# Layer 0 of a two-layer kernel: other buffers for the last tile's tokens and for fetched rows, other places for routing, statistics and expert halves

## The chip, the cores and the metric

The kernel runs on one core of one Trainium2 chip. A core has a matrix engine (TensorE, in the profile PE, with its weight loads as PEld), a vector engine (VectorE, DVE), an activation engine (ScalarE, ACT), a general engine (GpSimd, POOL) and a queue engine for transfers (SyncE, SP). Each engine works through its own queue in order. The metric is the device time of one execution in microseconds (us); the profile is of one execution of its own.

## The reference

There are 8 sequences of 512 tokens, 256 wide, all float32, and two layers. Each layer is an attention block and a feed-forward block, both behind a layer norm with a shift and a scale, and both added back through a gate.

```python
# layer 0, attention: a delta rule, one 16x16 state M per sequence and head, token after token
out_t = einsum('bnh,bnhd->bnd', q_t, M)
retrieved = einsum('bnhd,bnd->bnh', M, k_t)
M = M + b_t * einsum('bnh,bnd->bnhd', k_t, v_t - retrieved)
# layer 0, feed-forward: every token goes to the one expert of 8 with the largest logit
top_idx = argmax(x @ gate_w.T + gate_b + expert_bias)
out = w2[top_idx] @ relu(w1[top_idx] @ x + b1[top_idx]) + b2[top_idx]
# layer 1, attention: softmax(q k / 4 + relative bias, causal) v, 16 heads of 16
# layer 1, feed-forward: softmax over 8 experts, those under 0.1 dropped, all experts computed
```

## The kernel before

**Tiles and stages.** The 512 tokens of each sequence are cut into NT = 4 tiles of 128 tokens; a tile i of layer 0 holds 128 tokens of all 8 sequences. For each tile there are four stages.

- `front(i)`: layer norm, projections (L519, L523), silu, `squares` (the sums of squares for the L2 norm, L537 on DVE, waiting for `sq` of ACT, L533), `roots`, `scales` (the multiplications L572 on POOL), and `heads`, which transposes K and V into the order of the scan. Line 572 is in `scales`, lines 580 to 588 in `heads`.
- `scan(i)`: 128 dependent steps on DVE, four instructions each (L625, L629, L635, L640), which update the 128 states of 8 sequences and 16 heads at once. Four scans of this kind follow one another.
- `attend(i)`: what the tile's tokens read from the states: `deltas` (L659, transposes of V after the scan), and for each sequence b `turn`, `scores`, `mask`, `weigh`, `project` (L773, L777), `state`; then for each half h of four sequences `roots` (L804 on DVE, the reciprocal of a root that ACT took at L789), and for each b `rest` (L808, L811, L812, and L813, which stores x1 to memory) and `stats` (L820, L821: the statistics of the second layer norm).
- `route(i)` and `experts(i)`: `route` is a generator in six parts. Its two halves normalise four sequences each (L870, ACT), transpose them (L875), make logits (L893) and the tokens in their own order again (L899, L903). The additions L908, the choice of the expert, the counting matmul L928, the copy L933, the prefix matmuls (L935 to L940) and the comparison L948 follow, up to the slot numbers (L971) and the experts' row numbers `idx` (L980); then eight indirect transfers (L984, POOL) scatter the tokens to `hs`, sorted by expert. `experts` is a generator of 15 slots of 128 tokens in two halves: first half transposes of `hslot` (L1020), the first matmul (L1032) and its activations (L1041); second half the second matmul (L1050), `ysb` (L1055, L1056) and its store to `ys` (L1057). The weights come by indirect transfers on POOL (`fetch`, L1005, 1.05 MB for a first half and 1.18 MB for a second, two buffers for each). After the slots, `gather` (L1065) fetches each token's row back from `ys`; POOL multiplies it with the gate (L1094) and adds it to `x2d` in memory by an accumulating transfer (L1095). These rows lie in `yrow`, two buffers.

**Order.** `run(pieces, steps)` gives the order by hand. Each piece has a number; pieces are emitted in the order of their numbers, pieces with number s after step s of the running scan, and what a piece issues on DVE is put behind that step's L640 (`tc.issue_after`). On the other engines no such edge is set. A planner with costs of its own then fixes each engine's queue: in the trace the reciprocal L804 of the second half, with number 47, ran behind step 49 in scan 3 and step 51 in scan 2, and the zeroing of `v` (L207), emitted after the routing of the last tile, ran between two of its instructions.

While scan i runs, the pieces of `front(i + 1)`, of `attend(i - 1)`, `route(i - 1)` and `experts(i - 1)` run beside it, with those halves of experts that tile i - 2 had left over. `follow(i)` sets these places: the six parts of `route` (38, 47, 56, 61, 63 and 65), and the table `late, pace, starts`: the first `late` slots (10, for tile 2 it is 12) run at 73 + pace * slot in the same scan, a half every pace / 2, the others at `starts` and 3 later in the next. Scan 0 has only `front(1)` and small loads beside it. The last tile (i = 3) has no scan after it: its `attend` and `route` run after scan 3, with the last slots of tile 2 and the gathers of tiles 0 and 1, then its 15 slots with the gathers of tile 2 and with the first pieces of layer 1 (`prologue` of sequence 0: norm L120, transposes L179, values L244, and `both`, L261, the projections of q and k). In that stage the gathers stand at (1, 2.2) and (21, 2.2), which means number 1 and then every 2.2.

**Memory.** Pools take rooms of the on-chip memory one after another. `ap` holds the tiles of the scan and of attention (among them K and V of odd tiles, `terms`, `upd`, `dm`), and is closed in `place1`, where the pool `first1` (`bq`, `v`, `ew`, `qTc`) is opened on the side where other rooms have been given up.

**Layer 1** then goes through the sequences one by one: scores (L1243), bias (L1252), exponential (L1257), transposes (L1269), sums (L1290), with the tail of the sequence before beside it (experts at L1408).

## Time and profile before

| | |
|---|---|
| time, median of 3 runs | 2272.21 us (2269.37 to 2276.05) |
| profiled execution, its own time | 2273.54 us |
| profiled execution, span from the first to the last instruction | 2271.8 us |
| busy in the span | PE 1747.4, PEld 1204.0, DVE 1602.2, ACT 1063.0, POOL 646.9 us |
| mean granted clock of TensorE | 0.874 of full speed |
| first step of scans 0, 1, 2, 3 | at 64.8, 320.8, 588.7 and 869.2 us |
| last instruction of scan 3 on DVE | at 1120.62 us |
| first scores of layer 1 | at 1418.95 us |

The page gives for each engine the busy time, the span in 40 slices of 57 us with the busy share of each slice as a digit, the chain of waits that ended last, and groups of instructions by line. In the timeline a row has start, duration, engine, line, operation, names of what is written and read, the number of merged instructions, and in brackets the engine's idle time before it and what ended it. In the table by stretches, each engine has its busy time and number of instructions. In the list of waits a row has the waiting instruction, what it waited for, the sum, the number of times and the longest.

### The profile page before, as it was taken

Reading aid. Unit: us, or ns where it says so; the run is one execution under the profiler, and the core shown is the slowest. Engines: PE = TensorE matmul, PEld = TensorE weight load, DVE = VectorE, ACT = ScalarE, POOL = GpSimd, SP = SyncE. Lnnn points to the kernel's source line nnn. Section 1 sums busy time; section 2 is a strip of 40 time slices with the busy share of each in tenths; the row PEclk is TensorE's granted clock in tenths of the full one; section 3 lists DMA queues with packets and bytes.
Section 4 is the critical chain, followed back from the end, with each engine's and each line's share of the span. In section 5 each row is a group of like instructions: output and inputs, shape, how many; then the busy total and the mean of one; then the engine's idle time right before and its main releaser. Section 6 shows DMA issues by size and latency. Waiting matters only on the chain. (4 is left out here: it accounts for less than half of the span.)

```text
span 2271.8 us, 32168 instructions
## 1 busy us (share of the span) xinstructions
PE 1747.4 (77%) x10874; PEld 1204.0 (53%) x10874; DVE 1602.2 (71%) x4609; ACT 1063.0 (47%) x2571; POOL 646.9 (28%) x795
## 2 busy tenths in 40 slices
PE   5233026669687896869796787899999999999997
PEld 3212024448566685658775676555555555555553
DVE  3899999889997899999653001676676767666654
ACT  5144024554355543533332233878475666647431
POOL 1102016144472544743326643000102011110111
PEclk9667567689887998979997899899999999999998
DMA  5110000167313583238956884100101010100001
GB/s 160 47 44 9 0 1 10 36 214 278 142 54 98 198 292 121 80 110 317 268 120 162 278 309 141 42 8 15 19 15 24 15 27 12 24 13 13 17 17 17
DMA packets 88628, 214.11 MB, mean 94 GB/s; under 512 B 10872, under 2 KB 64288, under 8 KB 72848
## 3 DMA queue, kind: packets, MB, share of 16 engines
q0 software_dynamic: 33696, 161.98, 22.3%
q1 hardware_dynamic: 54768, 50.09, 7.6%
q8 instruction: 86, 1.41, 0.3%
q14 instruction: 78, 0.64, 0.1%
HBM read 175.10 MB, written 36.93 MB: 93 GB/s over the span
## 5 line engine op out<-in xcount | busy, mean ns | idle before, releaser
L1257 ACT ACTIVATE pr<-sc,low 128x384 f32<-128x384 f32 (+3 forms) x512 | 255.6, 556 | 196.5 <-DVE low L1252 194.2
L1032 PE MATMUL ps<-hTs,w 128*128 128x128 f32 x1920 | 250.7, 293 | 47.6 <-ACT hTs L1024 32.9
L1252 DVE CUSTOM_DVE_ANT_0 sc<-ps,strips 128x384 f32<-128x384 f32 (+3 forms) x512 | 225.4, 485 | 86.7 <-PE ps L1243 55.0
L1032 PEld LDWEIGHTS ps<-hTs,w 128*128 128x128 f32 x1920 | 239.2, 206 | 62.0 <-ACT hTs L1024 48.1
L629 DVE TENSOR_REDUCE state<-terms 128x16 f32<-128x272 f32 x512 | 227.3, 444 | 15.5
L1050 PE MATMUL ps<-w,act 128*128 128x256 f32 x960 | 223.3, 387 | 15.4 <-DMA w<-in_wrows,idx 12.6
L1408 PE MATMUL ps<-ew,hTd 128*128 128x512 f32 x512 | 232.9, 608 | 0.0
L640 DVE TENSOR_TENSOR state<-state,upd 128x256 f32<-128x256 f32 x511 | 220.6, 432 | 17.2
L635 DVE TENSOR_TENSOR upd<-K,state 128x256 f32<-128x256 f32 x511 | 213.9, 419 | 14.9
L1041 ACT ACTIVATE act<-ps,w 128x128 f32<-128x128 f32 x480 | 137.2, 369 | 186.1 <-PE ps L1032 104.7
L625 DVE TENSOR_TENSOR terms<-state,K 128x256 f32<-128x256 f32 x512 | 214.6, 419 | 11.9
L1050 PEld LDWEIGHTS ps<-w,act 128*128 128x128 f32 x960 | 182.1, 194 | 41.1 <-issue 13.9
L1269 PE MATMUL ps<-cst,pr 128*128 128x128 f32 x1280 | 191.5, 295 | 15.2 <-DVE low L1252 12.9
L1413 DVE SCALAR_TENSOR_TENSOR accd<-ps,wtd,accd 128x256 f32<-128x256 f32 x256 | 123.7, 483 | 101.4 <-PE ps L1408 89.5
L1269 PEld LDWEIGHTS ps<-cst,pr 128*128 128x128 f32 x1280 | 149.0, 148 | 83.9 <-DVE low L1252 24.7
L1417 POOL TENSOR_TENSOR accd<-accd,bc_g 128x256 f32<-128x256 f32 x32 | 23.2, 725 | 563.7 <-DVE accd L1413 563.7
L1408 PEld LDWEIGHTS ps<-ew,hTd 128*128 128x128 f32 x512 | 96.4, 193 | 121.2 <-issue 107.6
L1005 POOL DMA_INDIRECT w<-in_wrows,idx x120 | 117.3, 977 | 122.8 <-ACT act L1041 89.7
L1243 PE MATMUL ps<-kT,qTc 32*128 32x384 f32 (+3 forms) x1024 | 131.5, 492 | 6.3 <-DVE low L1252 4.4
L1278 DVE COPY prT<-ps 128x512 f32<-128x512 f32 (+3 forms) x256 | 117.0, 484 | 10.3 <-PE ps L1269 9.9
L725 POOL TENSOR_TENSOR stk<-stk,cst 128x512 f32<-128x512 f32 x96 | 119.3, 1270 | 17.1 <-ACT stk L724 15.1
L1276 ACT COPY prT<-ps 128x512 f32<-128x512 f32 (+3 forms) x256 | 99.0, 414 | 8.6 <-PE ps L1269 8.2
(252 smaller groups left out, 2878.7 us busy)
## 6 DMA issues: line engine op xcount, KB each, us to landing
hs<-zero SPq DMA_DIRECT2D x4, 1920.0 KB
hslot<-hs SPq DMA_DIRECT2D x60, 128.0 KB
ys<-ysb POOLq DMA_DIRECT2D x60, 128.0 KB, 3.1
x<-in_x SPq DMA_DIRECT2D x32, 128.0 KB
strips<-strip_d SPq DMA_DIRECT2D x16, 256.0 KB
out<-accd POOLq DMA_DIRECT2D x32, 128.0 KB, 3.1
wm<-in_wmod SPq DMA_DIRECT2D x4, 768.0 KB
xt<-in_x SPq DMA_DIRECT2D x12, 256.0 KB
```

Of the source, the lines that this page charges most:

```text
L625: nc.vector.tensor_mul(term[:, :, :HD], M, K[:, s, :].unsqueeze(1).to_broadcast([P, HD, HD]))
L629: nc.vector.tensor_reduce(delta, term, AX.X, ALU.add)
L635: nc.vector.tensor_mul(upd, K[:, s, :].unsqueeze(2).to_broadcast([P, HD, HD]), delta.unsqueeze(1).to_broadcast([P, HD, HD]),)
L640: yield nc.vector.tensor_sub(M, M, upd).ins
L1032: nc.tensor.matmul(ph[:, q * P : (q + 1) * P], w[:, k * FF + f * P : k * FF + (f + 1) * P], hT[:, k, :], start=(k == 0), stop=(k == 1),)
L1041: nc.scalar.activation(act[:, f, :], ph[:, q * P : (q + 1) * P], AF.Relu, bias=w[:, 2 * FF + f : 2 * FF + f + 1],)
L1050: nc.tensor.matmul(py[:, :D], act[:, f, :], w[:, f * D : (f + 1) * D], start=(f == 0), stop=(f == NFC - 1),)
L1243: made = nc.tensor.matmul(pscs[r][:, :W], qT[rows, g, o, i * P : (i + 1) * P], kT[rows, g, :W], start=True, stop=True,)
L1252: nc.vector.tensor_tensor_reduce(out=sc[:, :W], in0=pscs[r][:, :W], in1=strips[:, n, S - W :], scale=1.0, scalar=3.0e38, op0=ALU.add, op1= ...
L1257: nc.scalar.activation(pr, sc[:, :W], AF.Exp, bias=low, scale=-1.0)
L1269: nc.tensor.transpose(pt[:, (i - j) * P : (i - j + 1) * P], prs[r, i][:, j * P : (j + 1) * P], ident,)
L1408: nc.tensor.matmul(pe, hT[0][:, k, cols], ew[:, k, e : e + 2, :], start=(k == 0), stop=(k == 1),)
```

## The change

The numbers of pieces move. In `front`, for tiles 1 to 3, `squares` goes from +11 to +14 and `roots` and `scales` from +23 to +27; `heads` goes from 46 and 49 to 49 and 52. In `attend`, for tiles 0 and 1, `rest` and `stats` of the second half come 2 later and its `roots` 4 later. In `follow`, for tiles 0 and 1, the six parts of `route` go from (38, 47, 56, 61, 63, 65) to (38, 49, 59, 65, 69, 72), the first slot from 73 to 77, and the halves of left-over slots get places of their own, for tile 2 as well. The rows that are fetched back for tiles 0 and 1 go to eight parts of one buffer `fetched`, in the room of K, and the multiplication follows three gathers later and not one. For the last tile, the normalised tokens go to two scratch tiles in the rooms of `upd` and `dm`, and the tokens that are scattered to the room of `terms`, where both were written over x1. The two pieces `both` of the first three tiles of layer 1 go from 126 and 130 to 151 and 152.

```diff
@@ -600,13 +600,13 @@
                     late = 4.5 if i == 0 else 0
                     pieces.append((at + 8 * p + 3 * c + 4 + late, lambda b=b: project(b)))
-                    pieces.append((at + 8 * p + 3 * c + 11, lambda b=b: squares(b)))
+                    pieces.append((at + 8 * p + 3 * c + (14 if i else 11), lambda b=b: squares(b)))
             for h in range(B // n):
-                last = at + 16 * h + (23 if i else 39)
+                last = at + 16 * h + (27 if i else 39)
                 pieces.append((last, lambda h=h: roots(h)))
                 pieces.append((last + 2, lambda h=h: scales(h)))
-            pieces.append((at + 46, lambda: heads("K", qk[:, 1])))
-            pieces.append((at + 49, lambda: heads("V", v)))
+            pieces.append((at + 49, lambda: heads("K", qk[:, 1])))
+            pieces.append((at + 52, lambda: heads("V", v)))
             got["qk"] = qk
             return got, pieces
@@ -834,12 +834,15 @@
                     pieces.append((5 * b + 9, lambda b=b: state(b)))
                 pieces.append((5 * b + 8 + later, lambda b=b: project(b)))
             for h in range(2):
-                pieces.append((20 * h + 27, lambda h=h: roots(h)))
+                wait = 2 * h if i < NT - 2 else 0
+                pieces.append((20 * h + 27 + 2 * wait, lambda h=h: roots(h)))
                 for b in range(4 * h, 4 * h + 4):
-                    pieces.append((18 * h + 28 + b, lambda b=b: rest(b)))
-                    pieces.append((16 * h + 32 + b, lambda b=b: stats(b)))
+                    pieces.append((18 * h + 28 + wait + b, lambda b=b: rest(b)))
+                    pieces.append((16 * h + 32 + wait + b, lambda b=b: stats(b)))
             return got, pieces
+        DEPTH = (3, 3, 1, 1)
         issued = {}
@@ -859,6 +862,22 @@
                 return x.unsqueeze(1).to_broadcast([P, n, x.shape[1]])
             lg = grid("lg")
+            xn, made = h, h
+            if i == NT - 1:
+                xn = [
+                    ap.tile([P, HD, HD], F32, tag="upd", name=f"xnf{b}").rearrange(
+                        "p a b -> p (a b)"
+                    )
+                    if b % 2
+                    else ap.tile([P, 2, P], F32, tag="dm", name=f"xnf{b}").rearrange(
+                        "p a b -> p (a b)"
+                    )
+                    for b in range(2)
+                ] * (B // 2)
+                room = ap.tile([P, STEPS, HD, HD + 1], F32, tag="terms", name="h_last")
+                room = room.rearrange("p s a b -> p (s a b)")
+                made = [room[:, b * D : (b + 1) * D] for b in range(B)]
             for half in range(2):
                 rs, off = scale_offset(fp, "f", *norms[half])
                 pl = bank()
@@ -866,9 +885,9 @@
                 for n in range(5):
                     b = 4 * half + n
                     if n < 4:
-                        hb = h[b]
+                        hb = xn[b]
                         nc.scalar.activation(
-                            hb, hb, AF.Identity, bias=off[:, n : n + 1], scale=rs[:, n : n + 1]
+                            hb, h[b], AF.Identity, bias=off[:, n : n + 1], scale=rs[:, n : n + 1]
                         )
                         pt = bank()
                         for c in range(2):
@@ -900,9 +919,9 @@
                                 back[:, c * P : (c + 1) * P], turned[:, c, :], ident
                             )
                         if i == NT - 1:
-                            nc.vector.tensor_copy(h[b - 1], back[:, :D])
+                            nc.vector.tensor_copy(made[b - 1], back[:, :D])
                         else:
-                            nc.scalar.copy(h[b - 1], back[:, :D])
+                            nc.scalar.copy(made[b - 1], back[:, :D])
                     turned = hT
                 yield
                 nc.vector.tensor_add(
@@ -984,7 +1003,7 @@
                 issued["scatter"] = nc.gpsimd.indirect_dma_start(
                     out=hs_views[b],
                     out_offset=bass.IndirectOffsetOnAxis(ap=slot[:, b : b + 1], axis=0),
-                    in_=h[b],
+                    in_=made[b],
                     in_offset=None,
                 ).ins
             yield slot, idx
@@ -1082,17 +1101,24 @@
                         nc.gpsimd.dma_start(x2d[b][i], rows[b], accum_op=ALU.add)
                 yield
                 return
+            if i < NT - 2 and "fetched" not in w1:
+                fetched = ap.tile([P, P, HD], F32, tag="K", name="fetched")
+                w1["fetched"] = fetched.rearrange("p t d -> p (t d)")
             queue = []
-            for b in range(B + 1):
+            for b in range(B + DEPTH[i]):
                 if b < B:
-                    yr = fp.tile([P, D], F32, tag="yrow", name=f"yrow{i}_{b}", bufs=2)
+                    if i < NT - 2:
+                        yr = w1["fetched"][:, b * D : (b + 1) * D]
+                    else:
+                        yr = fp.tile([P, D], F32, tag="yrow", name=f"yrow{i}_{b}", bufs=2)
                     with tc.issue_after(issued["scatter" if i == NT - 2 else "fetch"]):
                         gather(b, yr)
                     queue.append(yr)
-                if b > 0:
-                    yr = queue.pop(0)
-                    nc.gpsimd.tensor_mul(yr, yr, gates[1][:, b - 1, :])
-                    nc.gpsimd.dma_start(x2d[b - 1][i], yr, accum_op=ALU.add)
+                if b >= DEPTH[i]:
+                    yr, k = queue.pop(0), b - DEPTH[i]
+                    nc.gpsimd.tensor_mul(yr, yr, gates[1][:, k, :])
+                    nc.gpsimd.dma_start(x2d[k][i], yr, accum_op=ALU.add)
                 yield
         def follow(i, qk, V):
@@ -1115,24 +1141,28 @@
             def on():
                 next(work["experts"])
-            pieces += [(38, begin), (47, more), (56, more), (61, more), (63, more), (65, settle)]
-
-            late, pace, starts = {
-                NT - 1: (0, 4, [10 * j for j in range(NSLOT)]),
-                NT - 2: (12, 4.3, [58, 68, 71]),
-                NT - 3: (10, 4.6, [10, 26, 44, 50, 66]),
-            }.get(i, (10, 4.6, [10, 26, 42, 58, 70]))
+            places = (38, 49, 59, 65, 69, 72) if i < NT - 2 else (38, 47, 56, 61, 63, 65)
+            pieces += zip(places, (begin, more, more, more, more, settle))
+            first, late, pace, starts = {
+                NT - 1: (0, 0, 4, [(10 * j, 10 * j + 3) for j in range(NSLOT)]),
+                NT - 2: (73, 12, 4.3, [(54, 64), (66, 67), (68, 69)]),
+                NT - 3: (77, 10, 4.6, [(9, 12), (22, 25), (35, 38), (58, 61), (70, 73)]),
+                NT - 4: (77, 10, 4.6, [(8, 11), (20, 23), (32, 35), (60, 63), (67, 70)]),
+            }[i]
             rest = []
             for j in range(NSLOT):
                 for half in range(2):
                     if j < late:
-                        pieces.append((73 + pace * (j + half / 2), on))
+                        pieces.append((first + pace * (j + half / 2), on))
                     else:
-                        rest.append((starts[j - late] + 3 * half, on))
+                        rest.append((starts[j - late][half], on))
             if i == NT - 1:
                 rest += [(200, on), (250, on)]
             at, apart = [(1, 2.2), (21, 2.2), (100, 2), (0, 0)][i]
-            return pieces, rest, [(at + apart * n, on) for n in range(B + 1)]
+            return pieces, rest, [
+                (at + apart * n, on) for n in range(B + DEPTH[i])
+            ]
         def load1():
@@ -1218,7 +1248,8 @@
         begun = list(prologue(0, first, w1["xs"], (tuple(range(NT - 1)), (NT - 1,))))
         for k, piece in enumerate(begun):
-            last.append((102 + 4 * k if k < NT + 4 else 201 + k, piece))
+            place = 102 + 4 * k if k < NT + 2 else 145 + k if k < NT + 4 else 201 + k
+            last.append((place, piece))
         run(last)
     rec.close()
```

## The prediction

> **What bounds the kernel now.** I read the table by stretches first, cut at the starts of scans 1, 2 and 3, at the end of scan 3 and at layer 1's first scores.
>
> ```profile
> core 0: us, PE busy (x) PEld busy (x) DVE busy (x) ACT busy (x) POOL busy (x), PEclk, DMA share, GB/s
> 320.80:588.70 267.90, 188.14 (x1214) 147.47 (x1213) 243.18 (x634) 132.40 (x324) 116.50 (x140) 0.80 0.39 135
> 588.70:869.20 280.50, 226.20 (x1528) 185.40 (x1527) 243.82 (x634) 142.94 (x371) 134.88 (x164) 0.89 0.44 154
> 869.20:1120.90 251.70, 197.04 (x1458) 168.38 (x1457) 232.27 (x592) 99.96 (x295) 121.68 (x141) 0.89 0.51 171
> 1120.90:1418.90 298.00, 232.88 (x1643) 198.80 (x1641) 56.02 (x146) 100.57 (x305) 142.88 (x166) 0.89 0.68 204
> ```
>
> In the scans DVE is the bound: 232 to 244 us busy, and scan 2 takes 12.6 us more than scan 1 for the same 634 instructions. Scan 3 has fewer of them. In the fourth stretch, 298 us, no engine is full, so a chain of waits sets the time. Layer 1 (853 us, PE busy 817) isn't touched; it starts earlier or later.
>
> Second view: the waits of DVE alone between 320 and 1120 us, which is what each scan loses.
>
> ```profile
> DVE ss L537 <- ACT sq L533: 12.0, 2, 6.4
> DVE ms L804 <- ACT ms L789: 11.4, 4, 7.0
> DVE lg L908 <- PE ps L893: 5.4, 2, 3.0
> DVE count L933 <- PE ps L928: 3.3, 2, 2.8
> ```
>
> With L948 (1.0) and L820 (0.5) that is 33.6 us. By scan, from the timeline of DVE: scan 1 L908 2.99, L933 0.53, L537 5.61, so 9.1; scan 2 L804 1.02 and 7.02, L820 0.46, L908 2.41, L933 2.80, L948 0.98, L537 6.42, so 21.1; scan 3 L804 1.20 and 2.16, so 3.4. In all of them DVE is in its queue too early for a result of PE and ACT, and the whole scan stands behind it.
>
> Third view: groups of POOL from 1131 to 1237 us, then three timelines of the same stage, for PE, DVE and POOL.
>
> ```profile
> L1065 POOL DMA_INDIRECT yrow<-ys,slot x16 | 16.9, 1054 | 25.8 <-DMA x<-yrow 25.1 <-issue 0.8
> L1095 POOL DMA_DIRECT2D x<-yrow x16 | 15.1, 966 | 5.4 <-POOL yrow L1094 4.0 <-issue 1.5
> L1094 POOL TENSOR_TENSOR yrow<-yrow,gate 128x256 f32<-128x256 f32 x16 | 13.0, 811 | 23.1 <-DMA yrow<-ys,slot 23.1
> ```
> ```profile
> 1205.50 1.18 PE L875 MATMUL ps<-cst,x 128*128 128x128 f32 x4 [11.59 <-ACT x L870]
> ...
> 1212.88 5.16 PE L1032 MATMUL ps<-hTs,w 128*128 128x128 f32 x32
> 1217.87 3.62 PE L1050 MATMUL ps<-w,act 128*128 128x256 f32 x16
> 1221.42 0.43 PE L928 MATMUL ps<-cst,pick 128*64 128x128 f32 x2
> ```
> ```profile
> 1225.23 0.22 DVE L980 TENSOR_SCALAR idx<-of,cst 128x15 uint32<-128x15 f32 x1
> ```
> ```profile
> 1237.03 1.00 POOL L984 DMA_INDIRECT hs<-x,slot  x1 [0.30 <-issue]
> ```
>
> POOL spends 106 us on 16 gathers, 54.3 us of them idle, nearly all waiting for one of two `yrow` buffers to be read or filled. So the scatter, ready at 1225.45, starts 11.6 us late. Ahead of it PE stood idle for 11.59 us before the second half of the routing and then ran two expert halves (8.6 us) between the logits and the count that the slot numbers need. Last, PE at the end of the stage:
>
> ```profile
> 1380.62 2.74 PE L261 MATMUL ps<-hTc,wqkv 128*128 128x384 f32 x8
> 1387.97 2.75 PE L261 MATMUL ps<-hTc,wqkv 128*128 128x384 f32 x8
> ...
> 1412.39 0.69 PE L179 MATMUL ps<-cst,xnc 128*128 128x128 f32 x2 [10.15 <-ACT xnc L172]
> ```
>
> The slots of the last tile follow one another there on PE without a wait (8.07 us each), and the two projections lie between them, while 10.15 us of idle stand behind the last slot.
>
> **The change, part by part.** The sum is made against the profiled execution's own 2273.54 us (span 2271.8 and 1.7 around it), which is 1.3 over the median.
>
> *A, places in the scans.* All stalls of scan 1 and those of scan 2 but the first L804 lie behind pieces that move: 9.1 + 20.1 = 29.2 us. A step is 1.91 us (290.2 to 305.5 for 8 steps). The second L804 comes 4 steps later, 7.6 against a stall of 7.02: gone. The additions L908 have six steps instead of five after the half that feeds them, 1.9 more against 3.0 and 2.4; I leave 1 us in each scan, +2. The copy L933 has 4 steps instead of 2, L948 3 instead of 2: both gone. `squares` comes 3 steps later, 5.7 against 5.6 and 6.4, and the last projection (number 78) no longer has three expert halves ahead of it but one, since the slots start at 77: gone.
>
> What comes back: in scans 2 and 3 two more expert halves stand before `project` of the fourth sequence (number 25): 8, 11, 20, 23 against 10, 13, and 9, 12, 22, 25 against 10, 13. Two halves are 8.2 us of PE (L1020 0.38, L1032 3.84, L1050 3.62 and gaps), and L804, just behind, has 1.0 and 1.2 us of stall already, with PE idle for about 2.5 us in that place in which part of it fits. The price is between 0 (the planner puts L804 as much later, as it did in scan 2, step 51 for number 47) and 8.2 in each scan; I take 3 and 2, near the rows of the present stall, because DVE has steps to run meanwhile: +5.
>
> The slots start later than at 77: the routing ends 7 steps later, 13.4 us, and the scatter (8 times 1.28) and the fetch stand behind that. In scan 1 the first L1032 goes from 480.4 to 480.4 + 13.4 - 3.5 (earlier stalls) = 490.3; the chain of ten slots lasted 97.6 us to 577.95 with two projections in it (4.5 each with their gaps), which now run before it: 490.3 + 88.6 = 578.9. PE needs V at 587.61 - 9.1 + 1 = 579.5. The 9.66 us that PE idled there are used up: no stall, but no cover; +1. In scan 2 the same sum ends 2 to 3 us ahead. `heads`, 3 steps later, end near step 104 of 128: 24 steps, 46 us of cover; the nearest wait, PE for POOL's `qk`, moves with it. A = -29.2 + 2 + 5 + 1 = -21, between -29 and -6.
>
> *B, routing of the last tile.* The first half of slot 12 (54) now stands before the second half of the routing, in the 11.59 us of idle; the second half (64) behind the prefix matmuls. The count then doesn't wait for 5.16 + 3.62: DVE had its operand at 1215.0, so 1221.42 becomes 1215.1, -6.3. If the tokens of slot 12 come late (they were issued at 1200.1 behind the stores of x1 on SP), L1032 runs in front of the routing instead and up to 5 us of this are lost. With eight places and a distance of three, POOL's own work is 16.9 + 15.1 + 13.0 + 32 issues of 0.3 = 54.6 us: free at 1132.4 + 55 = 1187 without waits, near 1200 if half of the 23.1 us for rows stays. From issue to landing these transfers took 2.7 to 14.6 us, median 4.1; three in flight at 3.4 us of POOL each cover 10. The second tile's gathers wait for the first tile's accumulation out of the same place, eight gathers or 27 us earlier: 0. Behind a gather that waits stand, on POOL, the fetches for slots 13 and 14 and the scatter. The first gather now waits for K's last reader (1119.7; it ran at 1132.43): 0.
>
> Ahead of the scatter stay on POOL the addition, store and fetch of slot 12, which follow L1050 (now 1216.6 to 1220.2): the scatter at 1224 instead of 1237, -13; with the risk of slot 12, -12. Behind it, slots 13 and 14 (PE to about 1237) and the first slot of the last tile (1255.68 - 12) still fit.
>
> [...]
>
> *Scratch and `terms`.* The normalisation needn't wait any more for the store of x1; but that L870 was ended by DVE's offset (1204.70), so 0. The third L870 of a half waits for the first transposes (0.6): +1 at most, in the risk above. `terms` is held until the scatter has read it, and `first1` may lie over it. Then the zeroing of `v` (L207, 1.76 us twice, which stood between the reciprocal and the offset of this routing) comes later, up to -3.5, and the loads of `ew`, 2 MB that ran at 1201 to 1210 at 301 GB/s, fall among the fetches of the last tile, whose first slots already waited 10.2 us for weights: up to +7. I take +3.
>
> *C.* Two `both` leave the row of slots: -2.74 - 2.75, and run in the 10.15 us of idle, beside ACT, which is idle too: -5.5, between -5.5 and -3 if they wait for ACT.
>
> Sum: -21 - 12 + 3 - 5.5 = -35.5; 2273.5 - 35.5 = 2238, at the median 1.3 less: 2236.5 us.
>
> **The rivals.** *The stalls come back at the front (0.14).* L804 of the first half takes the full 8.2 in scans 2 and 3, and L908 keeps its stall: A = -29.2 + 16.4 + 5 + 2 = -6, and the time 2252. For it: the granted clock of 0.8 to 0.89, which stretches PE's work. Against it: the longest such stall behind two halves was 7.0, the one at number 27 1.2.
>
> *The routing gains nothing (0.12).* The gathers go on waiting, or slot 12 is in front: B = 0 and the loads of `ew` +5: 2273.5 - 21 - 5.5 + 5 - 1.3 = 2250.5. This is also the case in which the change doesn't do what it says, one buffer in eight parts being treated as one. Against it: the eight gathers into parts of `rows` were issued 1.25 us apart at 1406.6 to 1415.4.
>
> *Slower (0.10).* The slots of tiles 0 and 1 run past the end of scans 1 and 2, and `deltas`, with all of `attend`, queues behind them. The lateness for each scan is 13.4 + 20 (ten slots at the 2 us of weight wait that the first five of the last tile had) - 9.66 = 24 us, 48 in all: 2284. It decides from 35.5 / 2 = 18 us for each scan. Against it: these slots followed one another at 8.07 us without a wait.
>
> **How the numbers follow.** Forecast 0.62; 0.14, 0.12 and 0.10 for the rivals; 0.02 for anything else. Its own best is A -29, B -16, C -5.5: 2221.5; its worst, with the first two rivals in part, is A -6, B -6, C -3, loads +5: -10, near 2262. The range is 2219 to 2262. A measurement here tells 0.3% (6.8 us) from no change: faster by that (under 2265.4) 0.84, within it 0.06, slower 0.10.
>
> **What would show it.** Right: scan 2 within 3 us of scan 1 with the waits for `sq` gone; the 16 gathers done by 1200 less the scans' gain; the scatter within 4 us of `idx`; L261 of 384 columns in the idle behind the last slot. Wrong: a wait at the first L804 over 5 us in scans 2 or 3; `deltas` behind slots in scan 2 or 3; L1032 of slot 12 directly before L875; waits of PE for weights over 15 us in the last tile's first five slots.

## The result, and the profile after

| | before | after |
|---|---|---|
| time, median of 7 runs each, in turn | 2270.58 us (2266.4 to 2277.12) | 2279.41 us (2276.44 to 2288.84) |
| ratio, with its 95% interval | | 1.0045 (1.0024 to 1.0066): slower |
| profiled execution, span | 2271.8 us | 2278.8 us |
| last step of scan 3 ends | 1120.1 us | 1138.2 us |
| first `deltas` of the last tile to layer 1's first scores | 288.2 us | 280.8 us |
| layer 1, from its first scores to the end | 852.8 us | 847.7 us |

The scans lost 18.1 us, the stage behind them won 7.4. Layer 1's 5.1 us are no part of it: over all profiles shown here it took 839.2 to 856.0 us with the same instructions.

In the kernel after, the lines from `route` on stand lower: L875 is L894, L893 L912, L908 L927, L928 L947, L933 L952, L948 L967, L980 L999, L984 L1003, L1005 L1024, L1020 L1039, L1032 L1051, L1050 L1069, L1056 L1075. The table by stretches of after, cut at its own scan starts (columns as before):

```profile
321.00:586.70 265.70, 185.56 (x1206) 144.92 (x1205) 242.35 (x634) 134.72 (x325) 114.41 (x137) 0.81 0.36 126
586.70:869.90 283.20, 216.79 (x1510) 177.80 (x1509) 242.60 (x633) 143.81 (x368) 134.01 (x163) 0.90 0.43 149
869.90:1138.40 268.50, 201.91 (x1476) 172.80 (x1475) 231.82 (x591) 101.79 (x301) 125.05 (x145) 0.85 0.51 172
1138.40:1431.10 292.70, 232.66 (x1651) 197.40 (x1649) 57.80 (x147) 100.77 (x305) 143.08 (x167) 0.90 0.70 210
```

DVE is as busy as before in each scan (242, 243, 232 us), so what the scans grew by is waiting: scan 3 takes 268.5 us instead of 251.7. The waits of DVE in the scans of after (waited for: sum, times, longest):

```profile
DVE ms L804 <- ACT ms L789: 16.6, 3, 8.0
DVE count L952 <- PE ps L947: 9.6, 2, 5.0
DVE dm L800 <- POOL bdM L801: 5.9, 3, 2.4
DVE ss L537 <- ACT sq L533: 5.1, 1, 5.1
DVE over L967 <- PE ps L959: 4.7, 2, 3.1
DVE ss L554 <- ACT ss L550: 4.6, 2, 3.3
```

Before had 12.0 us at L537, 11.4 at L804, 5.4 at L908 and 3.3 at L933. L537 and the logits shrank (L927, the old L908, has 3.4 us now), L804, the counting copy and the comparison (L967, before 1.0) grew, and two waits are new: L800 for POOL's state addition, and L554 (in `scales`) for the root of ACT.

Behind scan 3, the timelines of PE, DVE and POOL of after:

```profile
1220.04 0.69 PE L1039 MATMUL ps<-cst,hslot 128*128 128x128 f32 x2 [11.32 <-DMA hslot<-hs]
1221.19 6.31 PE L1051 MATMUL ps<-hTs,w 128*128 128x128 f32 x32 [0.46 <-ACT hTs L1043]
1227.34 0.60 PE L894 MATMUL ps<-cst,xnf 128*128 128x128 f32 x4
...
1276.57 0.69 PE L1039 MATMUL ps<-cst,hslot 128*128 128x128 f32 x2 [14.13 <-DMA hslot<-hs]
...
1423.95 0.69 PE L179 MATMUL ps<-cst,xnc 128*128 128x128 f32 x2 [5.00 <-ACT xnc L172]
```
```profile
1240.12 0.23 DVE L999 TENSOR_SCALAR idx<-of,cst 128x15 uint32<-128x15 f32 x1
```
```profile
1240.50 1.04 POOL L1003 DMA_INDIRECT hs<-h_last,slot  x1 [10.47 <-DVE idx L999]
```

POOL now waits for `idx` (10.47 us) and not the other way round: the scatter starts 0.15 us after it, as forecast. Slot 12 stands in front of the routing, with PE waiting 11.32 us for its tokens and computing 6.31. Even so `idx` is ready 90.0 us after the stage's first `deltas`, where it took 94.6 before, and the scatter starts after 90.2 us instead of 106.2. But the last tile's first slot then waits 14.13 us for its own tokens and starts after 126.3 us instead of 123.7.

### The profile page after: what moved, and what is told of

It is laid out like the page before. It is cut to its first block, busy times and chain, and to the rows that moved or that the text cites. A ratio compares the mean times of both kernels' runs of the same rounds, so it can differ in the third digit from the quotient of the medians.

```text
span 2278.8 us, 32182 instructions
## 1 busy us (share of the span) xinstructions
PE 1737.3 (76%) x10874; PEld 1193.4 (52%) x10874; DVE 1601.6 (70%) x4609; ACT 1070.3 (47%) x2576; POOL 647.0 (28%) x795
## 5 line engine op out<-in xcount | busy, mean ns | idle before, releaser
L1051 PE MATMUL ps<-hTs,w 128*128 128x128 f32 x1920 | 245.4, 289 | 46.7 <-ACT hTs L1043 37.2
L1051 PEld LDWEIGHTS ps<-hTs,w 128*128 128x128 f32 x1920 | 233.9, 203 | 62.0 <-ACT hTs L1043 53.7
L1069 PE MATMUL ps<-w,act 128*128 128x256 f32 x960 | 225.4, 389 | 16.7 <-DMA w<-in_wrows,idx 14.1
L640 DVE TENSOR_TENSOR state<-state,upd 128x256 f32<-128x256 f32 x511 | 220.8, 432 | 17.2
L1069 PEld LDWEIGHTS ps<-w,act 128*128 128x128 f32 x960 | 183.1, 196 | 41.8 <-issue 12.3
L1300 PE MATMUL ps<-cst,pr 128*128 128x128 f32 x1280 | 188.1, 291 | 15.5 <-DVE low L1283 12.1
L1300 PEld LDWEIGHTS ps<-cst,pr 128*128 128x128 f32 x1280 | 146.0, 146 | 84.1 <-DVE low L1283 24.6
L1024 POOL DMA_INDIRECT w<-in_wrows,idx x120 | 117.3, 977 | 168.8 <-ACT act L1060 139.4
L1274 PE MATMUL ps<-kT,qTc 32*128 32x128 f32 (+3 forms) x1024 | 131.6, 488 | 4.0 <-DVE low L1283 2.4
```

Source lines behind the costliest of these rows:

```text
L640: yield nc.vector.tensor_sub(M, M, upd).ins
L1051: nc.tensor.matmul(ph[:, q * P : (q + 1) * P], w[:, k * FF + f * P : k * FF + (f + 1) * P], hT[:, k, :], start=(k == 0), stop=(k == 1),)
L1069: nc.tensor.matmul(py[:, :D], act[:, f, :], w[:, f * D : (f + 1) * D], start=(f == 0), stop=(f == NFC - 1),)
L1274: made = nc.tensor.matmul(pscs[r][:, :W], qT[rows, g, o, i * P : (i + 1) * P], kT[rows, g, :W], start=True, stop=True,)
L1300: nc.tensor.transpose(pt[:, (i - j) * P : (i - j + 1) * P], prs[r, i][:, j * P : (j + 1) * P], ident,)
```

## The experiments

All kernels start from the diff's two sides and take some of its edits. The table collects what the traces of the main ones say: stalls are DVE's idle times over 0.3 us within a scan, "stage" is the time from the last tile's first `deltas` to layer 1's first scores. Each ratio is to the kernel before, measured beside it on the same chip.

| kernel | ratio (95%) | stalls in scans 1, 2, 3 | end of scan 3 | stage |
|---|---|---|---|---|
| before | | 9.1, 21.1, 3.4 | 1120.1 | 288.2 |
| after | 1.0045 (1.0024 to 1.0066) | 7.8, 24.6, 20.5 | 1138.2 | 280.8 |
| scans_only | 1.0067 (1.0042 to 1.0093) | 7.4, 24.4, 20.7 | 1136.8 | 289.4 |
| post_only | 0.9955 (0.9931 to 0.9979) | 8.9, 22.2, 5.5 | 1123.2 | 285.0 |
| scans_old_starts | 0.9967 (0.9941 to 0.9993) | 5.1, 12.9, 5.1 | 1110.5 | 289.4 |
| scans_starts_only | 1.0095 (1.0060 to 1.0129) | 7.8, 27.0, 16.2 | 1138.4 | 290.2 |
| change_old_starts | 0.9918 (0.9890 to 0.9946) | 5.3, 12.9, 4.6 | 1111.1 | 290.7 |
| starts_early | 1.0047 (1.0022 to 1.0072) | 7.4, 27.5, 9.2 | 1130.1 | 291.3 |
| starts_second | 1.0055 (1.0034 to 1.0075) | 8.1, 22.3, 12.1 | 1129.9 | 296.0 |
| starts_third | 1.0002 (0.9978 to 1.0027) | 8.1, 20.3, 5.9 | 1122.8 | 295.5 |
| warm_change | 1.0039 (1.0011 to 1.0066) | 5.2, 24.1, 17.2 | 1130.7 | 282.1 |
| rows_only | 0.9941 (0.9919 to 0.9963) | 8.0, 16.2, 4.6 | 1117.1 | 276.7 |
| both_only | 0.9945 (0.9920 to 0.9970) | 8.2, 13.0, 6.0 | 1115.8 | 285.5 |
| rows_both | 0.9917 (0.9888 to 0.9946) | 8.5, 20.3, 5.5 | 1125.0 | 271.2 |
| post_no_made | 0.9935 (0.9911 to 0.9959) | 8.4, 21.0, 5.5 | 1127.8 | 278.8 |

Stalls, end and stage come from one profiled execution of each kernel, and they vary. Seven kernels have all numbers in the scans as before (before, post_only, rows_only, both_only, rows_both, post_no_made and rows_both_64); their stalls are 8.0 to 9.1, 13.0 to 22.2 and 3.4 to 6.1 us. Seven have everything behind scan 3 as before (before, scans_only, scans_old_starts, scans_starts_only and the three starts_ kernels); their stages are 288.2 to 296.0 us. A difference inside such a spread shows nothing by itself.

**The two sides of scan 3.** scans_only has the edits to `front`, `attend` and the scans' part of `follow`; post_only the rest: slot 12's numbers, `fetched` with `DEPTH`, the scratch and `terms`, and `both`.

> The numbers of the scans alone (front, second half of attend, route, slots from 77, left-over slots); behind scan 3 all as before. First theory: the whole loss of scan 3 (17 us more stalls) and the slots that end behind scan 2 come from these numbers, so +16 to +20 us, about 2289, with scan 3 ending near 1139. Rival: the stalls of scan 3 come from what the planner makes of the pieces behind it, then under +8, about 2277.

> The changes behind scan 3 alone (eight places for the fetched rows at a distance of three, scratch and room of terms for the last tile, slot 12 at 54 and 64, both at 151 and 152); all numbers of the scans as before. First theory: the scans lost some 18 us and the last stage won, so here scan 3 ends at 1121 and the time is 7 to 12 us under the kernel before, about 2261. Rival: the last stage won only because the scans came late and the transfers beside it were done by then; then it stays within 3 us of the kernel before, about 2271.

Measured: 1.0067 and 0.9955. The places in the scans cost, the edits behind them gain, and the loss is larger than the gain.

**The numbers of the left-over halves.** Two theories: the new places of the halves that tile i - 2 left over crowd the early part of a scan; or the first ten slots, which start at 77 and later, run into the next scan.

```diff
 # scans_old_starts: scans_only, but (scans_starts_only is before with only the "-" lines' numbers)
-  NT - 3: [(9, 12), (22, 25), (35, 38), (58, 61), (70, 73)],
-  NT - 4: [(8, 11), (20, 23), (32, 35), (60, 63), (67, 70)],
+  NT - 3: [(10, 13), (26, 29), (44, 47), (50, 53), (66, 69)],
+  NT - 4: [(10, 13), (26, 29), (42, 45), (58, 61), (70, 73)],
 # change_old_starts: the whole change with the same two lines put back
```

> As scans_only, but the left-over slots of tiles 0 and 1 keep their numbers of before (10, 13, 26, 29, 42 or 44, ...); front, attend, route and the first slot at 77 moved. Theory late slots: scan 3's stalls come from slots that start at 77 and run past the end of scan 2, so deltas and all of attend start 6 us late; then scan 3 keeps 15 us or more of its 20.7 us of stalls, about +12. Theory left-over slots: they come from four halves before number 25 and six before 45; then scan 3 falls back to 3 to 7 us and the time to within 4 us of the kernel before.

> Only the left-over slots of tiles 0 and 1 at their new numbers, all else as before. Theory late slots: scan 3 stalls 3 to 7 us, time within 4 us of the kernel before. Theory left-over slots: scan 3 stalls 12 to 20 us, about +12, with the waits at L804 of the first half, the logits and the count, and deltas at once after the scans.

> The whole change, with the left-over halves of the first two tiles at their old numbers. If those numbers alone carry the loss, the stalls of scans 1, 2, 3 fall from 7.8 + 24.6 + 20.5 us to about 5 + 13 + 5, scan 3 ends 25 to 28 us earlier than in the kernel after, and the time is 2250 to 2256 us, ratio 0.992: the change turns from slower to faster by one table. If the loss came from the meeting of the scan places with what was added behind them (gathers, scratch, terms), stalls over 15 us stay in scans 2 and 3 and the time is 2268 us or more.

With the old numbers scan 3 falls from 20.7 to 5.1 us of stalls and scan 2 from 24.4 to 12.9; with only the new ones, 16.2 and 27.0 stand there. Scan 3 shows it best: in after its 20.5 us are 3.78 at the first L804, 3.75 at L800, 3.10 at the logits, 4.87 at the second L804 and 5.03 at the count, and in change_old_starts only the second L804 is left, with 4.55. And the whole change with two lines of its table put back is 0.8% faster than before instead of 0.45% slower. Its first ten slots still start at 77: they carry no loss. (Its profiled execution was the slowest of its six, 2270.1 us beside a median of 2256.8, so of that trace I read the scans and not the stage.) scans_starts_only lost 0.95%, some 22 us, more than the 12 expected, and its first L804 in scan 3 waited only 0.96 us. The wait that the late pair (58, 61) makes, in PE and DVE in scan 3 of scans_starts_only:

```profile
1008.16 5.23 PE L1051 MATMUL ps<-hTs,w 128*128 128x128 f32 x32
1013.22 3.62 PE L1069 MATMUL ps<-w,act 128*128 128x256 f32 x16
1016.77 0.43 PE L947 MATMUL ps<-cst,pick 128*64 128x128 f32 x2
```
```profile
1017.24 0.28 DVE L952 COPY count<-ps 64x128 f32<-64x128 f32 x1 [4.61 <-PE ps L947]
```

Both halves, 8.85 us of PE, went between the last logits and the counting matmul, where before PE was idle and the count came at once. It is the same pattern that the prediction had found, and priced at 6.3 us, in the last tile.

**Which half.** Before, with some of the new numbers alone: starts_early the first three pairs of each row, starts_second the second pair, starts_third the third.

```diff
 # starts_second                                          (starts_third)
-  NT - 3: [(10, 13), (26, 29), (44, 47), (50, 53), (66, 69)]
+  NT - 3: [(10, 13), (22, 25), (44, 47), (50, 53), (66, 69)]   # third: (26, 29), (35, 38)
-  NT - 4: [(10, 13), (26, 29), (42, 45), (58, 61), (70, 73)]
+  NT - 4: [(10, 13), (20, 23), (42, 45), (58, 61), (70, 73)]   # third: (26, 29), (32, 35)
```

> Before, with only the first three left-over slots of the first two tiles at the new numbers (8 to 38); the last two at the old ones (50, 53 and 66, 69; 58, 61 and 70, 73). If the loss comes from halves crowded ahead of the first half's projections and roots (numbers 20 to 38), the waits of DVE at the first reciprocal, at delta's multiplication and at the logits stay, some 11 of the 16.2 us of scan 3, only the wait at the slot comparison (4.6) goes, and the time is 2280 or more. If it is the halves at 58 to 63, in front of the counting, scan 3 falls to about 5 us and the time to within 5 of before.

> Before, with only the second left-over slot of tiles 0 and 1 earlier: (20, 23) and (22, 25) for (26, 29). The prediction's +5 came from this crowding (two more halves ahead of number 25). By it the first reciprocal waits longer in scans 2 and 3, 1.0 and 1.2 us become 2 to 5 each, and the time is some 5 us over before. If what is late is POOL (multiplication with the gate, ysb, store and fetch in one queue with the state additions), the wait stands at the statistics and at delta's multiplication of scan 2, steps 32 to 34, some 4 us, and the first reciprocal's goes. If the third slot carries all, the time is that of before.

> Before, with only the third left-over slot of tiles 0 and 1 earlier: (32, 35) for (42, 45) and (35, 38) for (44, 47). If a half in the steps 35 to 45 pushes the routing's matmuls and the state additions of POOL behind it, scan 3 gets the waits at delta's multiplication, the logits and the second reciprocal (some 8 to 9 us instead of 3.4), and scan 2, whose second reciprocal waited 7.0 us behind this very slot at its old place, gets no better (20 to 24). Time 5 to 8 us over before. If it is only freed of the slot in front of the roots, scan 2 falls to 14 and the time to 5 us under before.

Moving the second pair alone costs 0.55%, the third nothing that can be told, the three early pairs 0.47%, all five 0.95%. By subtraction about half of the loss is the second pair's and half that of the two last ones; but the intervals are wide, the two last pairs were not run alone, and of their share the traces show the 4.61 us at the count. What the second pair does stands in two views of starts_second, POOL's timeline in scan 2 and one line of DVE's:

```profile
655.10 1.43 POOL L811 TENSOR_TENSOR y<-y,gate 128x256 f32<-128x256 f32 x2
656.47 1.41 POOL L812 TENSOR_TENSOR x<-x,y 128x256 f32<-128x256 f32 x2
657.83 1.11 POOL L813 DMA_DIRECT2D x<-x  x2
658.96 0.73 POOL L801 TENSOR_TENSOR bdM<-bdM,dm 128x256 f32<-128x256 f32 x1
```
```profile
659.73 0.42 DVE L800 TENSOR_TENSOR dm<-ps,cst 128x256 f32<-128x256 f32 x1 [2.19 <-POOL bdM L801]
```

The planner put the reciprocal L804 behind step 31 instead of 27, and there it waits for nothing. But the multiplications, additions and stores that follow it (L811 to L813 for four sequences) came 4 steps later too, in POOL's queue, directly ahead of a state addition L801 (number 29), and the next L800 (number 34) stops the scan for 2.19 us, 2.21 in scan 3. Before, the same L801 stood behind them too, but it ended at 656.06, and L800 ran at 657.62 without a wait. In scan 3 L804 itself, at step 30, waits 2.42 as well, against 1.20 before. These three waits are 6.8 us of the 12 that the pair costs; where the rest is lost this trace doesn't show. I had expected the wait at L804 or at L800; it is at both. The starts_third theory of waits at the logits and at delta's multiplication held in scan 3 only for the logits (1.86 us), and its second reciprocal waited 3.52, which is no more than the 2.16 to 6.06 that it waits in the kernels with the old numbers; neither of the two times expected came.

**Is it the clock?** The same order of instructions need not give the same stalls. Over the first 75 steps of scan 2 the queues of PE, DVE, ACT and POOL have the same order in before, rows_only and both_only. DVE stalled there 14.7, 6.5 and 6.6 us, all of it in steps 24 to 75, and in these steps the granted clock stood at half for 41.0, 22.1 and 22.2 us. The half of a slot that the prediction's 7.0 us wait stood behind, in before and in both_only:

```profile
684.89 6.32 PE L1032 MATMUL ps<-hTs,w 128*128 128x128 f32 x32 [0.46 <-ACT hTs L1024]
```
```profile
679.54 3.84 PE L1051 MATMUL ps<-hTs,w 128*128 128x128 f32 x32 [0.52 <-ACT hTs L1043]
```

The second L804 then waits 7.02 us in before and 0.98 in both_only. All five kernels with the new second pair and no matmuls added have 41.0 us of half clock there, and after has 58.0 in the same steps of scan 3 (before 33.3). That made the clock a theory for the whole loss: halves that run early leave PE idle later, and the routing then runs at half clock. Opposite to it stands the queue: the halves are simply in front. warm_change adds matmuls to the change that nothing reads; warm_best adds them to best_front (below).

```diff
 # in route, each half of tiles 0 to 2: two behind the first transposes of half 0, four ahead of half 1
+  nc.tensor.matmul(pl, ident, cst[:, C_ID : C_ID + 512], start=True, stop=True)
```

> The whole change, with matmuls added that nothing reads (128x512, 1.11 us each at full clock): two behind the first transposes of the routing's first half, four ahead of its second half, for tiles 0 to 2. They lie where TensorE stood idle (3.5 and 6.6 us in scan 2, 13.6 us in scan 3). If the scans' stalls come from a TensorE that runs at half clock after such idle, the time at half clock in steps 24 to 75 falls from 41 us (scan 2) and 58 us (scan 3) to about 25 and 45, the stalls there from 18.2 and 20.5 us to about 8 and 13, and the time is near 2262 although TensorE has more to do. If the stalls come from work queued ahead on TensorE or GpSimd, the stalls stay or grow by the 2.2 us that were added, and the time is 2279 to 2285.

> front's numbers, eight places for rows, both in the idle, slot 12 at (58, 64), no scratch, and the same matmuls that nothing reads. If the clock sets the stalls, scan 2 loses about half of its 13.8 us in steps 24 to 75 and the time is 5 to 8 us under the same kernel without them (2248.8 beside a before of 2277), ratio 0.985 to 0.987. If not, it is the same or 2 to 4 us over it, 0.989 to 0.990.

The 23.9 us from 683.7 on, in which PE's clock was at half in after, in the table by stretches of after and of warm_change:

```profile
683.70:707.60 23.90, 19.81 (x92) 15.14 (x93) 14.81 (x43) 12.15 (x30) 8.95 (x11) 0.50 0.06 17
```
```profile
683.70:707.60 23.90, 19.43 (x106) 12.20 (x107) 19.04 (x58) 12.92 (x34) 10.97 (x15) 0.79 0.11 34
```

The clock did what the theory says: 0.79 instead of 0.50, half clock down from 41.0 to 23.9 us in scan 2 and from 58.0 to 40.5 in scan 3, and the second L804 waits 1.79 and 1.31 us instead of 7.96 and 4.87. The time didn't: 1.0039 against 1.0045, where 2262 us were expected and 2281.6 measured. The waits of DVE in warm_change, its lines from `route` on 10 lower again:

```profile
DVE count L962 <- PE ps L957: 10.0, 2, 5.4
DVE ms L804 <- ACT ms L789: 8.3, 4, 4.1
DVE dm L800 <- POOL bdM L801: 6.1, 3, 2.5
```

Count and L800 wait as long as ever, and the logits wait 2.04 and 2.19 us (0 and 3.10 in after). In steps 24 to 75 the stalls are 17.3 and 17.2 us instead of 18.2 and 20.5, while rows_only and change_old_starts, with about as much half clock (22.1 and 40.2, 19.5 and 36.8 us), have 6.5 and 4.6, and 5.5 and 4.6. So the clock decides how long the second L804 waits, but it isn't the cause of the whole loss; that theory fell. A smaller share isn't excluded: the two intervals leave room for some 9 us, the added matmuls may cost some time of their own, and in this profile scan 3 ends 7.5 us earlier than in after, while layer 1 takes 8.3 more. warm_best, 0.9890 (0.9846 to 0.9934) against 0.9884 for the same kernel without the matmuls, decides nothing: the 0.985 to 0.987 that the clock theory asked for lies inside its interval.

**Behind scan 3.** rows_only has `fetched` and `DEPTH` alone, both_only the new numbers of `both`; rows_both has these two, post_no_made slot 12's numbers as well. rows_both_64 is rows_both with slot 12's second half later.

```diff
-  DEPTH = (1, 1, 1, 1)                 # rows_only, rows_both
+  DEPTH = (3, 3, 1, 1)                 # with the eight places in the room of K
-  102 + 4 * k if k < NT + 4            # both_only, rows_both
+  102 + 4 * k if k < NT + 2 else 145 + k if k < NT + 4
-  NT - 2: [(58, 61), (68, 71), (71, 74)]
+  NT - 2: [(54, 64), (66, 67), (68, 69)]   # post_no_made; rows_both_64: (58, 64)
```

> Before, with only the eight places for fetched rows and the distance of three. POOL is then done with its 16 gathers some 20 us sooner and the scatter starts at idx, 11.6 us earlier against it: the stretch from deltas to layer 1's first scores is 276 to 278 us and the ratio 0.995. If the fetches of the last tile's weights, not the scatter, set the first slot, the stretch shrinks by less than 5.

> Before, with only the two projections of layer 1's second and third tile moved to 151 and 152. The prediction's part C by itself: 5.5 us from the stretch between the deltas of the last tile and layer 1's first scores (288.1 us), so 282 to 283 there and a ratio of 0.9976. If they only change places with other work, 288 and 1.0.

> Of the changes behind scan 3 only the eight places for fetched rows at a distance of three, and both at 151 and 152; no scratch, no room of terms, slot 12 at 58 and 61 as before; the scans as before. First theory: the scatter starts when idx is ready (-11.6 us), the slots of the last tile begin 9 to 12 us earlier, both saves 5: about 2257. Rival: the first slots of the last tile wait for their weights as long as the transfers before them take, and only both is won: about 2266.

> The changes behind scan 3 without the scratch tiles and the room of terms for the last tile's tokens; the scans as before. First theory: the pool of layer 1's first tiles no longer waits for the scatter, the 2 MB of ew load before it and not in front of the last tile's first hslot, so 8 to 12 us under post_only. Rival: the first slot waits for the fetches of weights, not for ew, and the time is that of post_only within 3 us.

> As rows_both, but slot 12 of tile 2 has its first half at 58 as before and its second at 64, behind the prefix matmuls, and slots 13 and 14 follow at 66 to 69. If the second matmul of slot 12 (3.6 us) is what holds the count up, the scatter comes 3 to 4 us earlier against deltas than in rows_both and the time is 3 us less; if the first slot of the last tile waits for its weights and not for the scatter, it is the same within 2 us.

rows_only shortens the stage from 288.2 to 276.7 us, 11.5, with the scatter right behind `idx`, and the time by 0.59%; the stage lies clear of the spread and the ratio's interval clear of 1. both_only's stage is 2.7 us shorter, and from rows_only to rows_both it is 5.5; its time fell by more (0.55%), but its scan 3 ended 4.3 us earlier and its layer 1 took 7.8 less with nothing changed there, so I don't put that down to the edit. With slot 12's new numbers the stage is 7.6 us longer (271.2 to 278.8), though the scatter starts as early (97.6 and 96.9 us after the first `deltas`); with (58, 64) it is 273.6 and the ratio 0.9921 (0.9888 to 0.9953), no better than 0.9917. With the scratch and `terms` it is 6.2 us longer still (278.8 in post_no_made, 285.0 in post_only). None of the steps of 2.7 to 7.6 us is clear of the spread (rows_both_front, with the edits of rows_both behind scan 3, has 276.7), and the times 0.9917, 0.9935 and 0.9955 don't tell these kernels apart.

What does stand out is the stretch from the scatter to the end of the stage's last second matmul. It is 173.2 to 178.6 us in the four kernels with the scratch and `terms` (after, post_only, change_old_starts, warm_change) and 156.9 to 167.9 in the sixteen without; the last tile's first slot waits 12.0 to 14.9 us in the four and at most 6.4 in the others. The two loads of `ew` on SP, in before and then in after, and PE's wait for that slot in before:

```profile
1201.17 1.34 SPq L212 DMA_DIRECT2D ew<-in_expert_w  x2
```
```profile
1253.86 1.01 SPq L212 DMA_DIRECT2D ew<-in_expert_w  x2
```
```profile
1254.53 0.69 PE L1020 MATMUL ps<-cst,hslot 128*128 128x128 f32 x2 [6.41 <-DMA hslot<-hs]
```

In before these loads were issued 36 us ahead of the scatter, in after 13 us behind its start, just ahead of the first slot's tokens (1254.98).

**Versions that beat both.** rows_both_front is rows_both with `front`'s four numbers; best_front the same with slot 12 at (58, 64); best_all has `attend`'s and `follow`'s new places on top, with the old left-over numbers.

> As rows_both, with the numbers of front moved as in the change (squares +14, roots +27, heads 49 and 52), and attend, route and slots as before. If squares waited because its number was too early by less than 6 us, the waits at L537 in scans 1 and 2 (12 to 15 us) go and the time is 8 to 12 us under rows_both, about 2248. If the planner moves the projection before it as well, the waits stay at 5 us each and the time is that of rows_both within 3 us.

> All places in the scans as the change has them but the left-over halves, with eight places for rows, a distance of three and both in the idle; no scratch for the tokens; slot 12 at (58, 64). The parts add: scan 3 ends at 1107 to 1111 us, the stretch from deltas to the first scores of layer 1 is 271 to 276 us, and the time 2240 to 2247. If the numbers in attend and follow bring stalls of their own (2.4 us more in scan 2 than front's numbers alone), it is 2 to 4 us slower than the kernel with front's numbers alone.

> As the one before, but of the places in the scans only front's. Scan stalls 5 + 10.5 + 6.5 us as in the kernel with front's numbers and slot 12 at (58, 61); time 2243 to 2248. If slot 12's later second half is worth its 5 us here too, 2243; if nothing, 2248.

Measured: 0.9902 (0.9865 to 0.9938), 0.9905 (0.9873 to 0.9937) and 0.9884 (0.9857 to 0.9912), that is 2248.8 us for best_front beside 2277.3 for the kernel before. They don't differ from one another by more than their intervals; all are about 1% faster than before. In best_all scan 3 ends at 1114.8 us and the time is 2251.7, both somewhat over what was expected; its stage of 274.4 is as expected.

## Why the prediction was wrong

It said 2236.5 us, 34 less than the 2270.6 that before took beside after (the sum had 35.5); it became 9 more. Of the marks in its own list, "L1032 of slot 12 directly before L875" came true in full, and "deltas behind slots" in scans 2 and 3 by 0.7 and 4.0 us; the first L804 stayed under 5 us (3.78 in scan 3), and PE's waits for weights in the last tile's first slots were 7.5 us.

- **A, what comes back: +5 for two more halves ahead of number 25.** This is the step that failed. The place and the first link were right: the second pair does delay L804, by 3 to 4 steps. It was taken that DVE then "has steps to run meanwhile" and the price ends at L804. The runs show POOL's share of `rest` sliding with it in front of L801. The second pair costs 0.55% (12 us) and all five pairs 0.95% (22 us), where +5 stood. The pairs at 58 to 63, to which the sum gave no price, stand in front of the count, which waits 5.03 us in scan 3 of after where it waited for nothing before. How the 22 us divide among the waits is shown only in part. Every one of the new pairs should have had the treatment that slot 12 had: what does it now stand in front of, on PE and on POOL?
- **A, the 29.2 us that were to go.** scans_old_starts has all the other new places and gained 0.33%, 7.5 us, not the 26 that the sum has without the +5. Three terms were mis-sized. The second L804 (7.02) was not a property of the order: with it unchanged the wait was 0.98 in both_only. Nor did it come 4 steps later in after: number 47 had run behind step 51, number 51 ran behind 52. The waits for `sq` did go in scans_old_starts (in after 5.15 us are left in scan 2), but there the next late thing is L554 behind ACT's root, 7.4 us in scan 2, as the waits of that kernel say:

```profile
DVE ss L554 <- ACT ss L550: 10.1, 2, 7.4
DVE count L952 <- PE ps L947: 4.0, 1, 4.0
```

  With `front`'s numbers alone (rows_both_front) neither L537 nor L554 waits in scan 2, but in best_front, with the same numbers in the scans, they wait 3.77 and 1.55 us. And L933 and L948, "both gone", are 9.6 and 4.7 us in after; 4.0 and 2.4 even with the old pairs. These 4.0 stand in scan 2, where the old table too has a pair at (58, 61).
- **A, slots end, +1, and the rival *slower*.** The first `deltas` came 0.69 and 3.96 us after the first step of scans 2 and 3, behind slots, where before they came 1.07 ahead of it. But scans_starts_only has the loss with -1.07 in both, and change_old_starts, with the slots from 77 on, has 0.68 and -0.87 and no loss. The rival had the sign and not the mechanism.
- **B, -12.** The term for the rows holds: rows_only took 11.5 us off the stage. In after the last of the 16 gathers was issued 55.0 us after the first `deltas` (97.5 before), and the scatter, 0.15 us behind `idx`, came 16.0 us sooner, more than the 13 forecast. The sign of the risk came true, slot 12's tokens came late and the half went in front of the routing, but `idx` was 4.6 us sooner all the same. Whether slot 12 took anything is open: the stage was 7.6 us longer with its numbers, with the scatter unmoved and inside the spread. Most of what the early scatter won was lost behind it, at the first slot's tokens, which is the term for the scratch.
- **Scratch and `terms`, +3 with a bound of +7.** Mis-sized: 6.2 us in the stage and 8.6 in the stretch behind the scatter (165.0 in post_no_made, 173.6 in post_only). The loads of `ew` went between the scatter and the first slot's tokens, as it said, and PE waited 14.13 us for these instead of 6.4. (The waits for weights before, 10.2 us in the prediction, are 8.6 by PE's waits: 7.1 at L1050 and 1.5 at L1032.)
- **C, -5.5.** PE's idle before L179 fell from 10.15 to 5.00, so the mechanism is right; the 2.7 to 5.5 us in the stage lie inside its spread.

So B, scratch and C together came to a ratio of 0.9955, 10 us, against the forecast's 14.5; A came to 1.0067, 15 us the other way, against 21. The rival *stalls come back at the front* put 16 us on the first L804, which waited 3.78 us at most, and on top of that kept the logits' stall; it had the sign of A's error, but the loss stood in waits behind that place.

## What to carry to other kernels

When a piece of work is moved into a hand-written order, ask of it what one asks of a wait that is removed: behind which matmul, and behind which addition, store or fetch of the general engine, does the waiting engine's next operand now stand. A wait taken from one profile may belong to that execution's clock and not to the order; look at the duration of the matmuls in front of it before counting on its whole length (here 7.02 us behind 32 matmuls that took 6.32, and 0.98 behind 32 that took 3.84). And put a table of numbers back line by line before dropping a change: two lines here turned 0.45% slower into 0.8% faster.

## What the runs showed of the hardware

- In the clock records of before, 50 of the 51 stretches at half clock lasted 3.41 us or a whole multiple of it (20 of 3.41, 12 of 6.83, 9 of 10.24, the longest 98.99; the last, at the end of the span, 6.71). One order of instructions got 41.0, 22.1 and 22.2 us of half clock over the same steps, 24 to 75 of scan 2, in the profiles of before, rows_only and both_only. At half, 32 matmuls of 128x128 took 6.32 us (before, at 684.89) instead of 3.84 (both_only, at 679.54). Stalls in steps 24 to 75 went with the time at half clock over the 18 profiles without added matmuls (a correlation of 0.94 in scan 2 and 0.93 in scan 3), yet in warm_change, with 17.1 and 17.5 us of half clock less than in after, the stalls fell only from 18.2 to 17.3 and from 20.5 to 17.2 us. A correlation over profiles didn't stand the test.
- In after, PE stood idle from 680.4 to 683.9 us and the clock was at half from 683.7 on for 23.9 us. In warm_change, PE's idle in the same place lasted 3.33 us; the fillers behind it took 3.68 us (1.98 in scan 3, at 966.57), and from 687.0 on pairs of the transposes took 0.38 us, where they took 0.63 in after (at 685.48).
